# Graph-network stack on one core: eigenvector setup and layer 0 issued in one order laid out by written durations, and the second batchnorm's end moved into layer 1

## The chip, the cores and the metric

The kernel runs on one core of one Trainium2 chip. The metric is device time in microseconds (us); the time before is the median of 3 runs. One execution was also recorded by the hardware profiler, and lines quoted as "profile" are from that record. The engines are PE (TensorE matmul), PEld (TensorE weight load), DVE (VectorE), ACT (ScalarE), POOL (GpSimd) and SP (SyncE, which issues the DMAs here). All data are fp32.

## The reference

The input x is 128 graphs x 64 nodes x 256 features; all graphs share one 64 x 64 adjacency matrix `adj`. Four layers are added to x, each behind a layernorm and a relu:

```python
h = maximum(layernorm(x), 0); x = x + L0(h, adj, ...)    # and so on for L1, L2, L3

def L0(f, A, W1, b1, g1, be1, W2, b2, g2, be2):          # mix, 256 -> 512 -> 256
    A_norm = A + eye; deg = A_norm.sum(0) + A_norm.sum(1) - diagonal(A_norm)
    A_hat = A_norm * rsqrt(deg)[:, None] * rsqrt(deg)[None, :]
    agg = einsum('nm,bmd->bnd', A_hat, f).reshape(-1, 256)
    h = relu(batchnorm(agg @ W1.T + b1, g1, be1))        # statistics over all 8192 rows
    return batchnorm(h @ W2.T + b2, g2, be2)             # the same

def L1(f, A, W1, b1, W2, b2):                            # 256 -> 128 -> 256 between U.T and U
    deg = A.sum(0) + A.sum(1) - diagonal(A)
    _, U = eigh(normalised(diag(deg) - A))
    h = relu(einsum('mn,bnd->bmd', U.T, f) @ W1 + b1)
    return einsum('nm,bmd->bnd', U, h @ W2 + b2)
# L2: two adjacency layers and four LSTMs over windows of nodes; L3: attention over 512 edges
```

## The kernel before

**Tiles.** The 8192 rows are cut into 16 blocks (`NB`) of 512 rows (`BT`, 8 graphs). Block i lives in the tile `X[i]` (128 x 4 x 256) from start to end. `big` holds layer 0's intermediate results, transposed (features on the partitions).

**Eigenvectors.** `begin` issues the loads of `adj`, its transpose and x. `adjacency` (L1353) computes degrees, the scaled matrix `S` and block-diagonal copies of A_hat (`BDH`) and of the adjacency (`BDA`), which mix two graphs in one matmul. `eigenvectors` (L1398) opens the solver `Fast`: `tridiagonal` (L883) takes 62 Householder steps, c = 63 to 2, each a chain of small operations that crosses PE, ACT and DVE: two matmuls for a row and a column of A (L905, L908); a square root, reciprocals and products for `NB`; `uA`, `KAP`, `uk`, `c2`, `v` from them; a matmul that keeps the reflector's row in the PSUM tile `VM` (L929, with the one-hot tile `hot`); two outer-product matmuls (L931, L932); the next row `x` (L937) with its sum of squares; and A's update (L941). Then `scale`, `reflectors`, `values`, `twisted` and `verdict` give `U` and a flag. A branch on the flag (`tc.If(bad > 0)`) holds a slower solver `Eig`, which was not run in this execution. After it `BDU` and `BDUT` are built from U and its transpose.

**Layer 0.** `layer0` (L1538) is emitted after the solver and before the branch, so that it runs beside the solver. Its first half goes over the blocks: `norms` for four blocks at a time, relu, mix with `BDH`, eight products with W1 (`ps<-z,w`), `bn_stats` of each result (L1577) and a copy. `bn_affine` then makes scale and shift of the first batchnorm. The second half goes over the blocks again: relu with scale and shift, a reload of `X[i]` (`load_x`), eight products with W2, `bn_stats` (L1590), a copy into `big`. After the second `bn_affine` a last loop over the blocks applies scale and shift on ACT (`big<-big`), and `add_transposed` (L1519) turns the block back with 8 transposes (L1525) into two PSUM tiles `pt`, which DVE adds to `X[i]`. PSUM pools: `l0ps` with 3 buffers, `l0tps` with 2.

**Order.** Engines take their instructions in the order in which the Tile framework's scheduler emits them. Between Householder steps and layer 0's first half that order is tied by hand: `tridiagonal` collects one matmul per step in `marks`, and `pace`, called by `Kernel.mm` (L1294), makes each layer-0 product depend (an order without a semaphore) on the mark that stands for its share of the columns.

**Layer 1.** `layer1` (L1601) goes over the blocks: `norm` (four `bn_stats`, four `bn_aggr`, small operations `n_v`, `n_y`, `n_r`, `n_m`, four relus `h`), eight products `BDU,h`, two copies `a`, products with W1 (`a,w`), relu `z`, and then twice for half a block: products with W2 (`w,z`) into a tile `pt`, `y` = that + bias, the product `y,BDUT` into another `pt`, and the add to `X[i]`. The pool `l1bps` gives `pt` 4 buffers:

```python
for jj in range(0, TPB, 2):
    p = ps2.tile([P, 2, D], F32, name="pt")
```

Layers 2 and 3 follow; the change doesn't touch them. Matmuls by `Kernel.mm` show as L1295 in the profile, activations as L1300, DVE helpers as L32 to L68.

Of the kernel before, what the change touches and what calls it, by code (L numbers as in the profile page):

```python
# [11 lines left out]
ALU = mybir.AluOpType  # L12
# [774 lines left out]

class Fast:
# [7 lines left out]
    def __init__(self, tc, ctx, k):  # L796
        self.tc, self.nc, self.k = tc, tc.nc, k
        self.o = Ops(tc.nc)
        self.pool = ctx.enter_context(tc.tile_pool(name="fast", bufs=1))
        self.rows = ctx.enter_context(tc.tile_pool(name="fastr", bufs=3))  # L800
        self.ps = ctx.enter_context(tc.tile_pool(name="fastps", bufs=2, space=PSUM))
        self.psv = ctx.enter_context(tc.tile_pool(name="fastvps", bufs=1, space=PSUM))
        self.tiles = {}
        self.marks = []
# [15 lines left out]

    def after(self, later, earlier):

        self.tc.add_manual_dep(later.ins, earlier.ins.name, mybir.DependencyInfo(
            mybir.DependencyClass.NoSync, mybir.DependencyReason.DATA), reason="issue order")
        return later
# [9 lines left out]
    def constants(self):  # L835
# [22 lines left out]

        self.hot = t("hot", 1, 127)
        nc.vector.memset(self.hot[:], 0.0)  # L860
        nc.vector.memset(self.hot[:, 63:64], 1.0)
# [21 lines left out]
    def tridiagonal(self, S):  # L883
# [4 lines left out]
        o.copy(m[:], self.mm((S, self.JR[:]))[:])  # L888
        o.copy(A[:], self.mm((self.JR[:], m[:]))[:])
        NB, OA, KAP = t("NB", 64, 64), t("OA", 64, 64, 2), t("KAP", 64, 64)  # L890
        nc.vector.memset(OA[:], 1.0)
        nc.vector.memset(KAP[:], 0.0)
        nc.vector.memset(NB[:], 0.0)
        s0, r, tt, q, c2 = (t("h_" + x, 64, 1) for x in "s0 r t q c2".split())
        VM = self.psv.tile([64, 64], F32, name="fvps")
        self.VM = VM
        ja = t("ja", 64, 64)
        bc = lambda c, n=64: c.to_broadcast([n, 64])
        x = self.rows.tile([64, 65], F32, name="f_x")
        o.copy(x[:, 0:63], self.mm((bc(ident[:64, 63:64]), A[:]))[:, 0:63])  # L900
        self.act(ja[:, 0:63], x[:, 0:63], AF.Square, accum_out=x[:, 63:64])
        for c in range(63, 1, -1):
            al, h = x[:, c - 1:c], x[:, c:c + 1]
            zp = self.ps.tile([64, 64], F32, name="fps")
            nc.tensor.matmul(zp[:, 0:c], bc(ident[0:c, c - 1:c], c), A[0:c, 0:c], start=True, stop=True)  # L905
            yp = self.ps.tile([64, 64], F32, name="fps")
            self.marks.append(
                nc.tensor.matmul(yp[:, 0:c], bc(A[0:c, c:c + 1], c), A[0:c, 0:c], start=True, stop=True))  # L908
            last = self.act(s0[:], h, AF.Sqrt)
            last = self.after(self.act(OA[:, c, 1:2], al, AF.Copy), last)  # L910
            z = self.rows.tile([64, 64], F32, name="f_z")
            self.after(self.act(z[:, 0:c], zp[:, 0:c], AF.Copy), last)

            o.ts(q[:], al, **halve(0))
            o.recip(r[:], s0[:])
            o.stt(tt[:], r[:], h, s0[:], ALU.mult, ALU.add)
            nb = NB[:, c - 1:c]
            o.mul(nb, q[:], tt[:])
            uA = self.rows.tile([64, 64], F32, name="f_uA")
            o.stt(x[:, c - 1:c + 1], OA[:, c, :], nb, x[:, c - 1:c + 1], ALU.mult, ALU.add)  # L920
            o.recip(KAP[:, c:c + 1], h)
            o.stt(uA[:, 0:c], z[:, 0:c], nb, yp[:, 0:c], ALU.mult, ALU.add)
            uk = self.rows.tile([64, 64], F32, name="f_uk")
            self.act(uk[:, 0:c], x[:, 0:c], AF.Copy, scale=KAP[:, c:c + 1])
            self.sum(c2[:], uA[:, 0:c], 0.5, uk[:, 0:c], ALU.mult)
            v = self.rows.tile([64, 64], F32, name="f_v")
            o.stt(v[:, 0:c], x[:, 0:c], c2[:], uA[:, 0:c], ALU.mult, ALU.subtract)

            nc.tensor.matmul(VM[:, 0:c], self.hot[0:1, 63 - c:127 - c], x[0:1, 0:c], start=c == 63, stop=c == 2)  # L929
            p = self.ps.tile([64, 64], F32, name="fps")  # L930
            nc.tensor.matmul(p[0:c, 0:c], uk[0:1, 0:c], v[0:1, 0:c], start=True, stop=False)  # L931
            nc.tensor.matmul(p[0:c, 0:c], v[0:1, 0:c], uk[0:1, 0:c], start=False, stop=True)  # L932
            if c > 2:
                xn = self.rows.tile([64, 65], F32, name="f_x")
                w = c - 1
                o.stt(xn[:, 0:w], uk[:, 0:w], v[:, w:c], z[:, 0:w], ALU.mult, ALU.add)
                row = nc.vector.scalar_tensor_tensor(xn[:, 0:w], v[:, 0:w], uk[:, w:c], xn[:, 0:w],  # L937
                                                     op0=ALU.mult, op1=ALU.add)
                self.act(ja[:, 0:w], xn[:, 0:w], AF.Square, accum_out=xn[:, w:c])
                x = xn  # L940
            rest = nc.vector.tensor_tensor(A[0:c, 0:c], A[0:c, 0:c], p[0:c, 0:c], op=ALU.add)  # L941
            if c > 2:
                self.after(rest, row)

    def reflectors(self):
# [4 lines left out]
        nc.vector.memset(V[:], 0.0)  # L950
        self.act(V[:, 0:63], self.VM[:, 0:63], AF.Copy)
# [290 lines left out]
    def vectors(self, S, U, UT):  # L1242
        o, nc, t = self.o, self.nc, self.t
        self.tridiagonal(S)
# [36 lines left out]
class Kernel:  # L1281


    def __init__(self, tc, ctx, io):
        self.tc, self.nc, self.ctx, self.io = tc, tc.nc, ctx, io
        self.o = Ops(tc.nc)
        self.const = ctx.enter_context(tc.tile_pool(name="const", bufs=1))
        self.copies = 0
        self.pace = None
# [4 lines left out]
    def mm(self, out, lhsT, rhs, start=True, stop=True):  # L1294
        m = self.nc.tensor.matmul(out, lhsT, rhs, start=start, stop=stop)  # L1295
        if self.pace:
            self.pace(m, rhs.shape[-1])
# [55 lines left out]
    def adjacency(self):  # L1353

        nc, o = self.nc, self.o
        with ExitStack() as cx:
            pool = cx.enter_context(self.tc.tile_pool(name="adj", bufs=1))
            psum = cx.enter_context(self.tc.tile_pool(name="adjps", bufs=2, space=PSUM))
            t = lambda n, *s: pool.tile([N, *s], F32, name="a_" + n)
            I = self.ident[:N, :N]  # L1360
            self.I2 = self.c("I2", N, P)
            o.copy(self.I2[:, 0:N], I)
            o.copy(self.I2[:, N:P], I)
            rs, cs, dg, deg, junk = t("rs", 1), t("cs", 1), t("dg", 1), t("deg", 2), t("junk", N)
            o.red(rs[:], self.A[:], ALU.add)
            o.red(cs[:], self.AT[:], ALU.add)
            o.stt(junk[:], self.A[:], 1.0, I, ALU.mult, ALU.mult, acc=dg[:])
            o.add(cs[:], cs[:], rs[:])

            o.sub(deg[:, 0:1], cs[:], dg[:])  # L1370
            o.ts(deg[:, 1:2], deg[:, 0:1], 1.0, ALU.add)
            di, dm, pos = t("di", 2), t("dm", 2), t("pos", 1)
            o.ts(dm[:], deg[:], 1e-30, ALU.max)
            self.rsqrt(pool, di[:], dm[:], "a_rt")
            o.ts(pos[:], deg[:, 0:1], 0.0, ALU.is_gt)
            o.mul(di[:, 0:1], di[:, 0:1], pos[:])
            dd = t("dd", 2, N)
            for i in range(2):
                o.ts(dd[:, i, :], I, di[:, i:i + 1], ALU.mult)

            An, Ah = t("An", N), t("Ah", N)
            o.add(An[:], self.A[:], I)
            p = psum.tile([N, N], F32, name="adj_ps")
            self.mm(p[:], An[:], dd[:, 1, :])
            o.ts(Ah[:], p[:], di[:, 1:2], ALU.mult)
            self.BDH = self.block_diagonal("BDH", Ah[:], psum)
            self.BDA = self.block_diagonal("BDA", self.AT[:], psum)

            L, self.S = t("L", N), self.c("S", N, N)
            o.add(L[:], self.A[:], self.AT[:])  # L1390
            o.ts(L[:], L[:], -0.5, ALU.mult)
            o.stt(L[:], I, deg[:, 0:1], L[:], ALU.mult, ALU.add)
            p = psum.tile([N, N], F32, name="adj_ps")
            self.mm(p[:], L[:], dd[:, 0, :])
            o.ts(self.S[:], p[:], di[:, 0:1], ALU.mult)
            self.U, self.UT = self.c("U", N, N), self.c("UT", N, N)

    def eigenvectors(self, beside):  # L1398

        nc = self.nc  # L1400
        with ExitStack() as ex:
            fast = Fast(self.tc, ex, self)
            fast.constants()
            left = fast.vectors(self.S[:], self.U[:], self.UT[:])
            beside(fast)
# [6 lines left out]
        with ExitStack() as cx:  # L1412
            psum = cx.enter_context(self.tc.tile_pool(name="adjps", bufs=2, space=PSUM))
            self.BDU = self.block_diagonal("BDU", self.U[:], psum)
# [31 lines left out]
    def norms(self, pool, blocks):  # L1446

        nc, o = self.nc, self.o
# [3 lines left out]
        for k, i in enumerate(blocks):  # L1452
            for j in range(TPB):
                nc.vector.bn_stats(st[:, TPB * k + j, :], self.X[i][:, j, :])
# [743 lines left out]
```

## Time and profile before

| what | value |
|---|---|
| runs | 2451.96, 2456.36, 2457.11 us; median 2456.36 |
| profiled execution | 2457.22 us, span 2455.4 us, mean granted clock 0.986 |
| busy share of the span | PE 95%, PEld 66%, DVE 66%, ACT 46%, POOL 0% |
| first Householder matmul; last update of A | 19.56 us; ends at 292.8 us |
| flag ready on DVE | 421.8 us |
| first matmul behind the branch | 432.4 us |
| last `y,BDUT` of layer 1 | starts at 585.9 us |
| first `BDA,h` of layer 2 | 612.4 us |

How to read it: times are from the start of the span. A row of the windows gives the stretch, its length, then for PE, PEld, DVE, ACT and POOL the busy time and the number of operations, the granted TensorE clock (1.00 is full speed), the share of time that the DMA engines were busy, and GB/s. A row of the timeline gives start, length, engine, line, operation, output <- inputs, partitions x elements and count; in brackets the engine's idle time just before and what released it. One matmul of this fp32 kernel shows as two records.

### The profile page before, as it was taken

Reading aid. Unit: us, or ns where it says so; the run is one execution under the profiler, and the core shown is the slowest. Engines: PE = TensorE matmul, PEld = TensorE weight load, DVE = VectorE, ACT = ScalarE, POOL = GpSimd, SP = SyncE. Lnnn points to the kernel's source line nnn. Section 1 sums busy time; section 2 is a strip of 40 time slices with the busy share of each in tenths; the row PEclk is TensorE's granted clock in tenths of the full one; section 3 lists DMA queues with packets and bytes.
Section 4 is the critical chain, followed back from the end, with each engine's and each line's share of the span. In section 5 each row is a group of like instructions: output and inputs, shape, how many; then the busy total and the mean of one; then the engine's idle time right before and its main releaser. Section 6 shows DMA issues by size and latency. Waiting matters only on the chain.

```text
span 2455.4 us, 31930 instructions
## 1 busy us (share of the span) xinstructions
PE 2342.8 (95%) x11925; PEld 1616.8 (66%) x11925; DVE 1630.4 (66%) x4147; ACT 1117.7 (46%) x2397; POOL 2.2 (0%) x15
## 2 busy tenths in 40 slices
PE   6888899798999999999999999999999999999989
PEld 3444444564777678888899999888885444444434
DVE  7656677885653778666677676657855465756467
ACT  3555554642433565444444444335635543443321
POOL 0000000000000000000000000000000000000000
PEclk9999999898999999999999999999999999999989
DMA  5000021121101000000100002000001000000001
GB/s 155 1 1 1 24 63 53 29 75 57 35 1 13 23 1 18 1 1 1 35 1 1 1 1 69 1 1 16 1 25 45 1 5 14 14 18 13 18 14 48
DMA packets 60086, 54.77 MB, mean 22 GB/s; under 512 B 14226, under 2 KB 57747, under 8 KB 59923
## 3 DMA queue, kind: packets, MB, share of 16 engines
q1 hardware_dynamic: 59922, 52.65, 6.9%
q8 instruction: 96, 1.57, 0.3%
q14 instruction: 68, 0.55, 0.1%
HBM read 35.86 MB, written 16.78 MB: 21 GB/s over the span
## 4 chain that ended last, share of the span: by engine, by line
PE 70%; DVE 3%; issue 1%; ACT 1%; DMA 0%; DVEq 0%; ACTq 0%
PE ps L1826 39%; PE ps L1295 22%; PE acc L1295 5%; PE pt L1295 2%; PE y L1295 1%; PE ps L2007 1%; DVE X L32 0%; DVE aw L32 0%; PE ps L1525 0%; ACT ls_g L1300 0%; DVE g L32 0%; DMA ls_w<-in_L_gnn_Wih_t_dram 0%; PE pt L1525 0%; DVE ls_g L32 0%; DVE n_st L1436 0%
## 5 line engine op out<-in xcount | busy, mean ns | idle before, releaser
L1300 ACT ACTIVATE ls_g<-ls_g,ls_b 128x512 f32<-128x512 f32 (+4 forms) x472 | 243.1, 565 | 154.9 <-DVE ls_g L32 153.1
L1300 ACT ACTIVATE ls_g<-ps,ls_b 128x256 f32<-128x256 f32 (+3 forms) x268 | 115.2, 470 | 328.5 <-PE ps L1826 324.5
L1295 PE MATMUL ps<-z,w 128*128 128x512 f32 x512 | 262.4, 638 | 0.1
L32 DVE TENSOR_TENSOR aw<-at,ed_OST 128x1024 f32<-128x1024 f32 x128 | 150.0, 1219 | 93.1 <-PE ps L1295 93.0
L1826 PE MATMUL ps<-ls_tx,X 128*128 128x160 f32 (+2 forms) x960 | 206.8, 326 | 1.2 <-DVE X L32 0.7
L32 DVE TENSOR_TENSOR ls_g<-ls_z,ps 128x512 f32<-128x512 f32 (+5 forms) x256 | 146.9, 579 | 91.2 <-PE ps L1826 89.7
L1826 PE MATMUL ps<-X,X 128*128 128x160 f32 (+1 forms) x896 | 199.0, 306 | 0.0
L1826 PE MATMUL ps<-X,ls_w 128*128 128x256 f32 x640 | 190.5, 379 | 0.0
L1826 PEld LDWEIGHTS ps<-ls_tx,X 128*128 128x128 f32 x960 | 161.7, 190 | 16.0 <-DVE X L32 5.8
L1826 PE MATMUL ps<-big,X 128*128 128x160 f32 (+2 forms) x720 | 160.4, 326 | 1.5 <-ACT ls_z L1300 1.3
L32 DVE TENSOR_TENSOR X<-ls_g 128x1024 f32<-128x1024 f32 (+2 forms) x108 | 117.4, 1087 | 50.5 <-ACT ls_g L1300 50.4
L1300 ACT ACTIVATE r<-ps 128x512 f32<-128x512 f32 x256 | 129.4, 625 | 42.0 <-PE ps L1295 41.7
L1826 PEld LDWEIGHTS ps<-X,X 128*128 128x128 f32 x896 | 148.5, 190 | 0.0
L1826 PE MATMUL ps<-X,ls_s 128*128 128x256 f32 x480 | 142.3, 379 | 0.0
L1295 PEld LDWEIGHTS ps<-z,w 128*128 128x128 f32 x512 | 90.0, 195 | 72.8 <-issue 62.6
L1826 PE MATMUL ps<-ls_tx,ls_s 128*128 128x256 f32 x464 | 134.7, 379 | 0.0
L1826 PE MATMUL ps<-ls_tx,ls_w 128*128 128x256 f32 x464 | 133.4, 380 | 0.0
L1826 PE MATMUL ps<-big,ls_w 128*128 128x256 f32 x464 | 131.9, 379 | 0.7 <-ACT ls_z L1300 0.7
L1826 PEld LDWEIGHTS ps<-X,ls_w 128*128 128x128 f32 x640 | 121.4, 190 | 16.8 <-DVE X L32 0.3
L1300 ACT ACTIVATE big<-ps 128x512 f32<-128x512 f32 x96 | 69.1, 754 | 138.9 <-PE ps L1295 81.8
L1826 PEld LDWEIGHTS ps<-big,X 128*128 128x128 f32 x720 | 121.5, 190 | 14.4 <-issue 7.4
L1295 PE MATMUL ps<-ed_S,Q 64*128 64x512 f32 x512 | 128.8, 617 | 1.4 <-DVE XV L65 1.3
(506 smaller groups left out, 4156.8 us busy)
## 6 DMA issues: line engine op xcount, KB each, us to landing
X<-in_x_dram SPq DMA_DIRECT2D x32, 512.0 KB, 4.3
xs<-X SPq DMA_DIRECT2D x16, 512.0 KB, 2.9
X<-xs SPq DMA_DIRECT2D x16, 512.0 KB, 3.9
out_dram<-X SPq DMA_DIRECT2D x32, 256.0 KB, 2.1
X<-in_L_gnn_Wih_t_dram SPq DMA_DIRECT2D x4, 512.0 KB, 3.5
ls_w<-in_L_gnn_Wih_t_dram SPq DMA_DIRECT2D x4, 512.0 KB, 4.3
ls_w<-in_L_gnn_Whh_t_dram SPq DMA_DIRECT2D x4, 512.0 KB, 5.9
w<-in_L_gnn_W_t_dram SPq DMA_DIRECT2D x2, 512.0 KB, 8.6
```

The source lines that it names most:

```text
L32: self.v.tensor_tensor(o, a, b, op=op)
L1295: m = self.nc.tensor.matmul(out, lhsT, rhs, start=start, stop=stop)
L1300: self.nc.scalar.activation(out, a, f, **kw)
L1826: self.nc.tensor.matmul(out, A[m][:, x, :], Bm[m], start=first and i == 0 and j == 0, stop=i == n - 1 and j == len(parts) - 1, skip_group_ ...
L2007: self.nc.tensor.transpose(p[:, j * P:(j + 1) * P], h[:, j, dc * P:(dc + 1) * P], self.ident[:])
```

## The change

- Instructions of PE, DVE and ACT are issued through wrappers (`Ordered`, `Engines`) that, while `ordered` is set, chain each engine's instructions in the order of emission.
- A `Plan` holds one list of steps. `chain` places a step of the main path at the time that its inputs and its engine allow, by durations written in the code; `beside` queues a step that is placed into a gap before a `chain` step when it fits with a slack of 0.6 us (PE) or 0.3 us (ACT, DVE). The steps are emitted in the order of their places. The main path is `adjacency`'s way to `S` and the Householder steps; beside it are `BDH` and all of layer 0's first half (`hidden0`). `marks`, `pace` and `after` are gone.
- The `VM` matmul and `hot` are gone: each step writes its reflector's row into the SBUF tile `V` with one DMA on SP's queue. The reciprocal `KAP` is issued before `uA` instead of after it. `f_x` has 4 buffers instead of 3.
- `BDA` is built after the branch.
- Layer 0's second half is `features0`, up to the second `bn_affine`, with the order left to the scheduler. `l0ps` has 5 buffers instead of 3; `l0tps` is gone.
- The last loop of layer 0 becomes `end0(i)`, called at the head of block i in `layer1`, with its transposes in `l1bps`, that is in the tiles `pt` of layer 1.

The core of the diff:

```diff
+class Ordered:
+        def call(*a, **kw):
+            i = method(*a, **kw)
+            if self.owner.ordered:
+                if self.last is not None:
+                    self.owner.tc.add_manual_dep(i.ins, self.last.ins.name, mybir.DependencyInfo(
+                        mybir.DependencyClass.NoSync, mybir.DependencyReason.DATA), reason="issue order")
+                self.last = i
+            return i
...
+class Plan:
+    def start(self, x):
+        needs, at = list(x.needs), self.free[x.engine]
+        if x.bank is not None and len(self.opened) >= self.banks:
+            needs += self.opened[-self.banks]
+        for y in needs:
+            if y.at is None:
+                return None
+            at = max(at, y.at + y.ready)
+        return at
+
+    def fill(self, engine, until):
+        while True:
+            best = None
+            for x in self.queue[engine][:12]:
+                at = self.start(x)
+                if at is not None and at + x.busy <= until + self.slack[engine] and (best is None or at < best[0]):
+                    best = at, x
+            if best is None:
+                return
+            self.queue[engine].remove(best[1])
+            self.place(best[1], best[0])
+
+    def chain(self, engine, emit, needs=(), busy=0.09, ready=0.22):
+        x = Step(engine, emit, needs, busy, ready, None)
+        self.fill(engine, max([y.at + y.ready for y in needs], default=0.0))
+        self.place(x, self.start(x))
+        return x
...
-            nc.tensor.matmul(VM[:, 0:c], self.hot[0:1, 63 - c:127 - c], x[0:1, 0:c], start=c == 63, stop=c == 2)
...
+        def row_uk():
+            nc.sync.dma_start(V[c:c + 1, 0:c], now["x"][0:1, 0:c])
+            now["uk"] = self.rows.tile([64, 64], F32, name="f_uk")
+            self.act(now["uk"][:, 0:c], x(0, c), AF.Copy, scale=KAP[:, c:c + 1])
...
+        z = go("T", zy, [rest], 0.34, 0.42)
+        sq = go("S", lambda: self.act(s0[:], x(c, c + 1), AF.Sqrt), [h], 0.13, 0.23)
...
+        d = go("V", lambda: o.recip(KAP[:, c:c + 1], x(c, c + 1)), [d])
+        uk = go("S", row_uk, [d], 0.16, 0.32 + e)
+        d = go("V", row_uA, [zs, b, z], 0.12 + e, 0.25 + e)
...
     def eigenvectors(self):
+            plan = Plan(dict(T=0.6, S=0.3, V=0.3), 5)
+            made, mixes = self.adjacency(fast, plan)
+            self.open0(ex)
+            self.hidden0(plan, mixes)
+            fast.tridiagonal(self.S[:], made, plan)
+            nc.ordered = True
+            plan.emit()
+            nc.ordered = False
+            left = fast.vectors(self.U[:], self.UT[:])
+            plan.rest()
+            plan.emit()
+            self.features0()
             bad = nc.values_load(left[0:1, 0:1], min_val=0, max_val=64)
...
+            self.BDA = self.block_diagonal("BDA", self.AT[:], psum)
             self.BDU = self.block_diagonal("BDU", self.U[:], psum)
...
+    def hidden_block(self, i, r, m, plan, needs, used):
...
+            x = beside("T", lambda hc=hc: product(hc, 0), mixed, 0.86, 0.9, bank)
+            x = beside("T", lambda hc=hc: product(hc, 1), [x], 0.86, 1.0)
+            used[i].append(x)
+            bank.append(beside("V", lambda hc=hc: nc.vector.bn_stats(self.st1[:, hc, i, :], now["p", hc][:]), [x],
+                               0.62, 0.7))
+            bank.append(beside("S", lambda hc=hc: self.act(self.hidden(i, hc), now["p", hc][:], AF.Copy),
+                               [x] + h, 0.55, 0.65))
...
-            for i in range(NB):
-                for oc in range(2):
-                    self.act(self.part(i, oc), self.part(i, oc), AF.Identity,
-                             scale=sc2[:, oc:oc + 1], bias=sh2[:, oc:oc + 1])
-                self.add_transposed(pst, i, lambda dc, j: self.part(i, dc)[:, j * P:(j + 1) * P])
...
+    def end0(self, i, psum):
+        sc2, sh2 = self.affine2
+        for oc in range(2):
+            self.act(self.part(i, oc), self.part(i, oc), AF.Identity, scale=sc2[:, oc:oc + 1], bias=sh2[:, oc:oc + 1])
+        self.add_transposed(psum, i, lambda dc, j: self.part(i, dc)[:, j * P:(j + 1) * P])
...
     def layer1(self):
             for i in range(NB):
+                self.end0(i, ps2)
                 h = self.norm(pool, i)
```

## The prediction

> **What bounds the kernel now.** The sum is made against the profiled execution: 2457.2 us, of which the span is 2455.4; the median of the runs, 2456.4, lies 0.8 lower. About 0.2% (5 us) is what a measurement of this kernel can tell from no change.
>
> First the windows by stage. The columns are the stretch, its length, then busy time and count for PE, PEld, DVE, ACT and POOL, the granted clock, the DMA share and GB/s.
>
> ```profile
> 20.00:293.00 273.00, 232.13 (x1133) 122.54 (x1132) 184.06 (x968) 145.74 (x539) 0.00 (x0) 0.97 0.05 15
> 293.00:432.00 139.00, 132.35 (x391) 58.24 (x391) 106.67 (x445) 70.59 (x122) 0.00 (x0) 0.98 0.21 62
> 432.00:456.00 24.00, 16.29 (x95) 12.10 (x96) 19.80 (x52) 19.71 (x29) 0.00 (x0) 0.79 0.06 18
> 456.00:586.00 130.00, 124.70 (x554) 83.04 (x553) 99.16 (x342) 57.65 (x117) 0.74 (x3) 0.99 0.19 63
> ```
>
> The rows are the Householder steps beside layer 0's first half; the values beside its second half; the 128 transposes that end layer 0; layer 1. PE is 85, 95, 68 and 96% busy. Layer 1 has no slack on PE, and gets there by overlapping blocks. That is seen in its timeline (start, length, engine, line, operation, count, idle before):
>
> ```profile
> 573.73 1.13 PE L1295 MATMUL pt<-w,z 128*128 128x256 f32 x4
> ...
> 574.70 1.05 PE L1295 MATMUL ps<-BDU,h 128*128 128x128 f32 x8
> 574.90 0.69 DVE L32 TENSOR_TENSOR y<-pt,w_b 128x512 f32<-128x512 f32 x1 [0.26 <-PE pt L1295]
> ...
> 575.64 1.12 PE L1295 MATMUL pt<-y,BDUT 128*128 128x512 f32 x2
> ...
> 576.81 0.69 DVE L32 TENSOR_TENSOR X<-X,pt 128x512 f32<-128x512 f32 x1 [1.22 <-PE pt L1295]
> ```
>
> While DVE makes y, PE works at another block's BDU,h: the wait from w,z to y,BDUT (1.91 us) costs PE little, because a later block's norm is ready. Next the clock around the branch, in windows with the same columns:
>
> ```profile
> 428.00:432.00 4.00, 0.44 (x2) 0.00 (x0) 0.70 (x1) 0.60 (x1) 0.00 (x0) 1.00 0.01 4
> 432.00:436.00 4.00, 1.09 (x4) 0.93 (x4) 3.21 (x17) 0.20 (x1) 0.00 (x0) 0.53 0.29 82
> 436.00:440.00 4.00, 2.39 (x9) 1.62 (x10) 1.38 (x5) 3.51 (x5) 0.00 (x0) 0.50 0.05 19
> 440.00:444.00 4.00, 3.57 (x20) 2.92 (x19) 3.83 (x9) 4.00 (x7) 0.00 (x0) 0.69 0.00 0
> ```
>
> Behind 4 us without PE work the clock stands at half, and it is full again only near 443, 5 us after the transposes began at 437.4.
>
> **Start.** The first Square stands at 20.15 us, behind S at 17.44. The new order puts adjacency first: A lands at 2.96; some 17 small DVE operations, a square root and seven dependent operations at 0.15 to 0.2 bring S to about 8.3; the 2.7 from S to Square stay. 11.0 instead of 20.15: -9.
>
> **Householder steps.** 62 steps from 20.0 to 292.6 are 4.40 us each. Timeline of one of them:
>
> ```profile
> 101.69 1.12 PE L1295 MATMUL ps<-z,w 128*128 128x512 f32 x2
> ...
> 102.74 0.28 PE L931 MATMUL fps<-f_v,f_uk 1*47 1x47 f32 x2
> ...
> 103.40 0.31 PE L905 MATMUL fps<-f_A,ident 46*64 46x46 f32 x2 [0.29 <-DVE f_h_q L47]
> ```
>
> The step's matmuls stand behind layer-0 products; the dependent operations alone add up to 3.19 in this stretch (v to x 0.29, x 0.29, square 0.30, root 0.36, NB 0.23 + 0.19 + 0.25, x 0.26, KAP 0.22, uk 0.18, c2 0.38, v 0.24). The built order of the changed kernel has four steps without products (3.19 each, and about 4 for the first 16 bn_stats of 0.36 that stand among them: 17), 45 that carry all of layer 0's first half, two without (bn1; 8.5 together), 11 with second-half products. The 45: PE needs 8 products x 0.86 + 2 mixes x 0.98 = 8.84 per block, 141 us for 16, 3.14 per step, with 0.65 for the step's own matmuls 3.8; small misfits of DVE and ACT make it 4.15, 187 us. The 11: about 45, 4.1 each. 11 + 17 + 187 + 8.5 + 45 = 268, rounded down to 266 since the last steps are short. Gain 27, the start's 9 included. Bounds: 3.8 per filled step and 3.2 at the end give 243 (gain 50); one product of 0.86 too many in each of the 45 gives 305 (loss 12).
>
> The VM matmul becomes one DMA per step on SP. Its x tile returns four steps (16 us) later, and the slowest DMA kind in the page's list lands after 8.6: hidden, 0. V's last row lands some 2 us late, beside `scale`.
>
> **Values.** DVE's chain took 129.2 us (292.6 to 421.8). It loses 8 of 28 bn_stats (-3.4) and takes the layer-3 edge work and X0's adds (+9.5) which stood behind the branch: 135, and 4 to the branch: 139 as before (139.8). All second affines lie before the branch too, on ACT, in the twisted loop. If that cover is gone they cost 32 x 0.73 = 23 at most. The branch moves from 432.4 to about 405.4.
>
> **Layer 1.** This decides. Each block's head now has two X adds and 8 transposes, into the `pt` ring that layer 1's w,z and y,BDUT use. Ring tiles are handed out in program order, so the built order puts the transposes of block i+1 behind the last y,BDUT of block i; its norm needs those adds, and its BDU,h the norm. On PE, DVE and ACT the 16 blocks stand strictly one after the other: nothing fills the links. The links, from the start of a last y,BDUT, by rows of layer 1, the transposes and the norms at 605 to 612:
>
> - X add +1.17, next block's two X adds 0.60 apart; bn_stats at 2.97 (the transposes, 1.16 for eight, end at 2.1 under these adds);
> - four bn_stats and aggr, n_v at 4.70; n_y 0.17, reciprocal 0.24, five operations at 0.19: n_m at 6.07; first h at 6.25, four relus 0.51 apart, last ready at 8.36;
> - BDU,h and copy a to 10.40; a,w to z 1.06; z to w,z 0.74; w,z to y 1.17; y to y,BDUT 0.74: 14.11;
> - second w,z +0.97, y +1.06, y,BDUT +0.74: 16.9.
>
> So P = 16.9 us per block at full clock, though PE has only 7.45 + 1.16 = 8.6 to do. PE idles from 2.1 to about 7 in each block, longer than the 4 us that halved the clock above. The matmuls in the chain during the 5 us of recovery, half of BDU,h (1.05) and a,w (0.86), take as long again, with a little of w,z: +2.1, P = 19.0. Bounds: +0, and all the chain's matmuls at half clock, +6.4, P = 23.3.
>
> [...]
>
> Before, 153.5 us lay between the branch and the last y,BDUT (432.4 to 585.87), transposes included. After, block 0's transposes lie before the branch; its bn_stats start some 2.1 us behind the branch, 2.97 into a period: 16 P - 0.9. The loss is 16 P - 154.4, at 19.0 us 150. The rest of the kernel keeps its order. Sum: 2457.2 - 27 + 150 = 2580.
>
> **Rivals.**
> - The clock stays full, P = 16.9: loss 116, 2546. For it: small gaps elsewhere in the Householder stage leave the mean clock at 0.97.
> - The clock stays at half, P = 23.3: loss 218, 2649. For it: PE would be half idle. Against it: near 443 the clock was restored by transposes that left PE idle a fifth of the time.
> - The Householder steps do not shorten (the written durations miss, each engine waits in turn): 2607.
> - Other side, faster: blocks overlap as before, a few ahead; then PE's 8.6 per block is the price, 16 x 8.6 - 154.4 = -17, with -27: 2413. Place: layer 1 alone; it decides below P = 11.3, where 16 P - 154.4 = 27. Against it stands the built order, which holds no matmul of block i+1 ahead of block i's last.
>
> **How the numbers follow.** Forecast 0.50, full clock 0.25, half clock 0.10, no Householder gain 0.10, overlap 0.05. The range 2520 to 2640 runs from the full clock with the Householder gain near its bound (2523) to the forecast with a small Householder loss or P near 22; it leaves out the overlap and most of the half-clock case. Faster 0.05, within 0.2% 0.01, slower 0.94.
>
> **What would show it.** Right: last Householder add near 266, branch near 405, layer 1 with PE about half busy, BDU,h of a block 9 us behind the previous y,BDUT, clock of 0.6 to 0.8 there. Wrong: PE over 75% busy in layer 1, or BDU,h between w,z and y,BDUT of another block; a Householder end past 292.

## The result and the profile after

The changed kernel takes 2591.3 us (median of 4 runs, 2589.9 to 2592.2), the kernel before 2456.6; the ratio is 1.0552, 95% interval 1.0534 to 1.0570. Slower was forecast, at 2580. The profiled execution took 2589.9 us, its span is 2588.1: 132.7 more than the span before. In the table a stage ends at the start of the operation named; "predicted" is from the text above.

| event (us from the span's start) | before | predicted | after |
|---|---|---|---|
| first square of a Householder row | 20.15 | 11.0 | 11.35 |
| last update of A | 292.6 | 266 | 285.6 |
| first matmul behind the branch | 432.4 | 405.4 | 421.6 |
| last `y,BDUT` of layer 1 | 585.9 | 708.5 | 721.0 |
| from the branch to it | 153.5 | 303.1 | 299.4 |
| first `BDA,h` of layer 2 | 612.4 | not given | 746.6 |
| from there to the end | 1843.0 | the same | 1841.5 |

So 10.8 us are gained up to the branch, layer 1 loses 145.9, and the rest differs by -2.4: 132.7. In the changed kernel nearly all instructions show as L798, the line of the wrapper that issues them. First the windows, with the columns as above: the Householder steps, the values, layer 1, four pieces of one period of layer 1, and the stretch at half clock of the period behind it.

```profile
15.40:286.00 270.60, 247.33 (x1099) 126.48 (x1100) 198.53 (x998) 173.47 (x577) 0.00 (x0) 0.98 0.13 37
...
286.00:421.00 135.00, 89.43 (x302) 40.87 (x300) 107.72 (x472) 63.59 (x112) 0.74 (x3) 0.84 0.12 34
421.00:721.00 300.00, 181.22 (x640) 118.61 (x640) 118.23 (x355) 57.03 (x112) 0.00 (x0) 0.85 0.09 28
...
498.00:503.00 5.00, 0.09 (x1) 0.09 (x1) 3.64 (x17) 0.94 (x3) 0.00 (x0) 1.00 0.31 105
503.00:506.00 3.00, 3.00 (x13) 2.95 (x14) 0.69 (x1) 1.34 (x3) 0.00 (x0) 0.50 0.00 0
506.00:509.00 3.00, 2.60 (x9) 1.05 (x7) 0.00 (x0) 0.96 (x2) 0.00 (x0) 0.93 0.00 0
509.00:516.00 7.00, 5.06 (x20) 2.97 (x20) 2.77 (x5) 0.32 (x1) 0.00 (x0) 1.00 0.00 0
...
520.10:526.90 6.80, 5.66 (x19) 4.58 (x20) 1.02 (x3) 2.67 (x5) 0.00 (x0) 0.50 0.00 0
```

PE's share in layer 1 went from 96 to 60%, and part of that 60% is half clock: each period has 5 us without PE work, and near their end the clock falls to 0.50, for 3.4 us in this period (503.0 to 506.4) and for 6.8 in the next. No other engine took PE's place as the bound; all three wait in turn. The values stage is 66% PE now, with DVE the busiest at 80%. The timeline of one period shows the links (start, length, engine, line, operation, count, idle before):

```profile
502.26 2.08 ACT L798 ACTIVATE h<-X,n_m,n_r 128x256 f32<-128x256 f32 x4 [1.30 <-DVE n_m L798]
...
502.91 3.81 PE L798 MATMUL ps<-BDU,h 128*128 128x128 f32 x16 [5.17 <-ACT h L798]
...
509.38 1.13 PE L798 MATMUL pt<-w,z 128*128 128x256 f32 x4 [0.78 <-ACT z L798]
510.54 0.69 DVE L798 TENSOR_TENSOR y<-pt,w_b 128x512 f32<-128x512 f32 x1 [4.63 <-PE pt L798]
...
511.29 1.12 PE L798 MATMUL pt<-y,BDUT 128*128 128x512 f32 x2 [0.79 <-DVE y L798]
...
514.06 1.13 PE L798 MATMUL pt<-y,BDUT 128*128 128x512 f32 x2 [0.78 <-DVE y L798]
...
515.02 1.04 PE L798 MATMUL pt<-ident,big 128*128 128x128 f32 x8
```

Between `w,z` and `y,BDUT` stood another block's BDU,h before; now PE idles there (0.79), and for 5.17 us ahead of BDU,h, released by the relu `h` of the same block. The next block's transposes (515.02) stand behind the last product of this one. The DVE rows `n_m`, one per block, stand 18.31 and 19.23 us apart in turn, 18.8 on average; the longer period is the one with 6.8 us at half clock.

### The profile page after: what moved, and what is told of

It is laid out like the page before. It is cut to its first block, busy times and chain, and to the rows that moved or that the text cites. A ratio compares the mean times of both kernels' runs of the same rounds, so it can differ in the third digit from the quotient of the medians.

```text
span 2588.1 us, 31946 instructions
## 1 busy us (share of the span) xinstructions
PE 2355.6 (91%) x11801; PEld 1627.5 (63%) x11801; DVE 1639.5 (63%) x4145; ACT 1118.8 (43%) x2396; POOL 2.2 (0%) x15
## 4 chain that ended last, share of the span: by engine, by line
PE 67%; DVE 3%; ACT 0%; issue 0%; DMA 0%; SPq 0%; DVEq 0%; ACTq 0%
PE ps L798 59%; PE acc L798 5%; PE pt L798 2%; DVE sm_m L798 1%; PE y L798 1%; DVE X L798 0%; DVE aw L798 0%; DVE n_st L798 0%; ACT ls_g L798 0%; DVE g L798 0%; DVE ls_g L798 0%; DMA X<-in_L_gnn_Wih_t_dram 0%; DMA ls_w<-in_L_gnn_Wih_t_dram 0%; DVE sm_e L798 0%; DVE ls_s L798 0%
## 5 line engine op out<-in xcount | busy, mean ns | idle before, releaser
L798 ACT ACTIVATE ls_g<-ls_g,ls_b 128x512 f32<-128x512 f32 (+4 forms) x472 | 243.1, 565 | 154.6 <-DVE ls_g L798 152.6
L798 ACT ACTIVATE ls_g<-ps,ls_b 128x256 f32<-128x256 f32 (+3 forms) x268 | 115.2, 470 | 328.7 <-PE ps L798 324.8
L798 PE MATMUL ps<-z,w 128*128 128x512 f32 x512 | 254.8, 624 | 0.0
L798 PE MATMUL ps<-big,X 128*128 128x176 f32 (+3 forms) x848 | 212.8, 366 | 0.5 <-ACT ls_z L798 0.4
L798 DVE TENSOR_TENSOR aw<-at,ed_OST 128x1024 f32<-128x1024 f32 x128 | 149.8, 1218 | 92.3 <-PE ps L798 92.3
L798 PE MATMUL ps<-ls_tx,X 128*128 128x160 f32 (+2 forms) x960 | 206.7, 326 | 1.2 <-DVE X L798 0.6
L798 DVE TENSOR_TENSOR ls_g<-ls_z,ps 128x512 f32<-128x512 f32 (+5 forms) x256 | 146.6, 578 | 91.5 <-PE ps L798 90.0
L798 PE MATMUL ps<-X,X 128*128 128x160 f32 (+1 forms) x896 | 199.0, 306 | 0.0
L798 PE MATMUL ps<-X,ls_w 128*128 128x256 f32 x640 | 190.4, 379 | 0.0
L798 PEld LDWEIGHTS ps<-ls_tx,X 128*128 128x128 f32 x960 | 161.8, 190 | 15.9 <-DVE X L798 5.5
L798 PEld LDWEIGHTS ps<-big,X 128*128 128x128 f32 x848 | 145.9, 190 | 30.5 <-issue 19.4
L798 DVE TENSOR_TENSOR X<-ls_g 128x1024 f32<-128x1024 f32 (+2 forms) x108 | 117.4, 1087 | 50.9 <-ACT ls_g L798 50.8
L798 PEld LDWEIGHTS ps<-X,X 128*128 128x128 f32 x896 | 148.5, 190 | 0.0
L798 ACT ACTIVATE r<-ps 128x512 f32<-128x512 f32 x256 | 129.4, 625 | 41.8 <-PE ps L798 41.7
L798 PE MATMUL ps<-X,ls_s 128*128 128x256 f32 x480 | 142.3, 379 | 0.0
L798 PE MATMUL ps<-BDU,h 128*128 128x128 f32 x256 | 62.1, 436 | 81.9 <-ACT h L798 81.9
L798 PE MATMUL ps<-ls_tx,ls_s 128*128 128x256 f32 x464 | 134.7, 379 | 0.0
L798 PEld LDWEIGHTS ps<-z,w 128*128 128x128 f32 x512 | 88.8, 192 | 72.5 <-issue 63.6
L798 PE MATMUL ps<-ls_tx,ls_w 128*128 128x256 f32 x464 | 133.3, 380 | 0.0
L798 PE MATMUL ps<-big,ls_w 128*128 128x256 f32 x464 | 131.9, 380 | 0.7 <-ACT ls_z L798 0.7
L798 PEld LDWEIGHTS ps<-X,ls_w 128*128 128x128 f32 x640 | 121.4, 190 | 16.8 <-DVE X L798 0.3
L798 PE MATMUL ps<-ed_S,Q 64*128 64x512 f32 x512 | 128.6, 617 | 1.4 <-DVE XV L798 1.3
```

Source lines behind the costliest of these rows:

```text
L798: i = method(*a, **kw)
```

## The experiments

**Theory.** The end of the second batchnorm in layer 1 makes layer 1 serial, because its transposes share the ring `pt` (the 4 buffers of that pool, handed out in turn) with layer 1's products and so stand behind the block before; the clock that falls in the gap costs some 2 us per block; the rest of the change gains. **Rivals:** the written order itself slows the kernel; the place in the program makes it serial, not the ring; the clock costs nothing and the links are only longer than the rows said. Ratios are to the kernel before, run on the same chip.

### Layer 1

`e1_end0_first`: the loop goes back ahead of layer 1, the rest of the change stays.

```diff
+            cx0, (pst,) = self.stage([("l0tps", 2)])
+            with cx0:
+                for i in range(NB):
+                    self.end0(i, pst)
             self.layer1()
...
-                self.end0(i, ps2)
```

> Edit: the changed kernel, but all 16 end0 calls stand ahead of layer 1, in a PSUM pool of their own (as before the change); everything else of the change stays. Theory 1 (end0 at the block's head, through the shared ring, makes layer 1 serial at P = 18.8 us per block): layer 1 falls from 299.5 us, branch to last y,BDUT, to about 150 (153.5 before the change), and the time from 2591 to about 2445, some 11 below the kernel before, which is what the Householder and values part gains. Rival (the loss sits in the static order or in a clock that the new order leaves low for the whole stage): layer 1 stays above 200 us, the time above 2500.

Measured: 2437.5 us, ratio 0.9932 (0.9909 to 0.9955); branch to last `y,BDUT` 148.6 us, layer 1's PE full again (97% busy from 447 to 571 us).

`e2_own_ring`: the same place, another ring.

```diff
-        cx, (w, pool, psum, ps2) = self.stage([("l1w", 1), ("l1", 2), ("l1ps", 4), ("l1bps", 4)])
+        cx, (w, pool, psum, ps2, pst) = self.stage([("l1w", 1), ("l1", 2), ("l1ps", 3), ("l1bps", 3), ("l1tps", 2)])
...
-                self.end0(i, ps2)
+                self.end0(i, pst)
```

> Edit: end0 stays at the head of each block of layer 1, but its transposes get a ring of their own (2 buffers; l1ps and l1bps have 3 instead of 4). Theory 1 with the ring as the cause: the transposes no longer wait for y,BDUT, blocks overlap, layer 1 takes 130 to 155 us, the time is 2425 to 2450. Rival (the place in the program alone makes it serial: norm(i+1) is emitted behind block i): P stays near 18.8, 2590. A second rival: 3 buffers instead of 4 hold layer 1 back, 160 to 200 us, 2450 to 2490.

Measured: 2435.4 us, ratio 0.9927 (0.9904 to 0.9949). All 128 transposes now stand ahead of the branch, which moves to 437.5, and layer 1 takes 127.6 us. So neither the place in the program nor 3 buffers cost much: the shared ring did.

`e3_two_ahead`: the shared ring, two blocks of lead.

```diff
-                self.end0(i, ps2)
+                for k in (range(3) if i == 0 else range(i + 2, min(i + 3, NB))):
+                    self.end0(k, ps2)
```

> Edit: the shared ring stays, but end0 is called two blocks ahead (blocks 0 to 2 ahead of block 0, then block i+2 at the head of block i). Theory 1 in the form of the chain (what costs is that block i+1's norm hangs on transposes behind block i's last product): with two blocks of lead the norm is ready in time, P falls to PE's or DVE's own work, 8.6 to 10 us, layer 1 to 140 to 160, the time to 2430 to 2455. Rival (sharing 4 buffers among six tiles per block is the cost by itself, whatever the lead): P above 12, the time above 2490.

Measured: 2433.8 us, ratio 0.9921 (0.9898 to 0.9944); layer 1 takes 142.1 us, 8.9 per block with its start counted in. The window of that stage:

```profile
424.00:566.00 142.00, 132.66 (x625) 91.81 (x625) 109.64 (x351) 55.94 (x112) 0.00 (x0) 0.96 0.18 59
```

PE is at 93%, with the same work in half the time. Six tiles per block in four buffers are no cost by themselves; what cost is that a ring hands out its tiles in program order, and that the norm hung on a tile handed out behind the last product of the block before.

`e5_before_moved`: the kernel before, with this part of the change alone.

```diff
-            sc2, sh2 = self.bn_affine(w, "bn2", st2, b2, g2, be2)
-            for i in range(NB):
-                ...
+            self.affine2 = self.bn_affine(self.const, "bn2", st2, b2, g2, be2)
...
             for i in range(NB):
+                self.end0(i, ps2)
                 h = self.norm(pool, i)
```

> Edit: the kernel before, with only one part of the change: the second batchnorm's scale, shift, transposes and adds go to the head of each block of layer 1, through the shared ring; adjacency, Householder steps and layer 0 stay as they were. Theory: this part alone makes layer 1 serial: from the branch to the last y,BDUT 295 to 305 us instead of 153.5, the time 2457 + 146 = 2600, give or take 8. Rival (the serial layer 1 needs the changed kernel's emission order): under 2500.

Measured: 2608.3 us, ratio 1.0629 (1.0608 to 1.0650); branch to last `y,BDUT` 307.9 us, in the same periods of 18.31 and 19.23. The loss needs nothing else of the change. The 8.5 us over layer 1 of the changed kernel lie at its start, where the second batchnorm's scale and its first block still come behind the branch: the first `y,BDUT` follows it after 24 us instead of 15.

### The clock

`e4_warm`: 44 transposes of the identity more per block, in a `ps` tile that nothing reads.

```diff
                 self.end0(i, ps2)
+                p = psum.tile([P, BT], F32, name="ps")
+                for k in range(44):
+                    self.nc.tensor.transpose(p[:, k % 4 * P:(k % 4 + 1) * P], self.ident[:], self.ident[:])
```

> Edit: the changed kernel with 44 more transposes of the identity per block in layer 1, into a ps tile that nobody reads; the scheduler puts 21 of them (about 3 us) behind a block's 8 transposes, where PE idles, and the rest into the waits for z and y. Theory 1 with the clock term (P = 16.9 at full clock, the rest of 18.8 is half clock behind the gap): granted clock in layer 1 near 1.00, P near 16.9, the time falls by 16 x 1.9 = 30 to about 2561. Rival (the links are longer than the rows said, and the clock costs nothing): the same or slower than 2591.

Measured: 2583.6 us, ratio 1.0529 (1.0505 to 1.0553); 8 less, not 30; the interval overlaps that of the changed kernel, and layer 1 in the profile is 5.1 us shorter (294.3). Neither side was right as written. Two blocks of its timeline:

```profile
503.13 3.65 PE L798 MATMUL ps<-BDU,h 128*128 128x128 f32 x16 [2.88 <-ACT h L798]
...
521.90 2.19 PE L798 MATMUL ps<-BDU,h 128*128 128x128 f32 x16 [2.89 <-ACT h L798]
```

After the same pause the 16 records took 3.65 us in one block, near the 3.81 of the changed kernel (502.91, where the windows read 0.50), and 2.19 in another, about twice the 1.05 that eight take in the kernel before (574.70, in a window at 0.99): behind a pause of 2.9 us the products came once at about half rate and once at full. The granted clock is 0.92 from 424 to 716 us, where the changed kernel has 0.86 from 424 to 721. Three of fifteen periods are 17.36 or 17.37 us, the others 18.5 to 19.1.

`e6_warm_gap`: all 44 in the gap, by taking the extra tile from the shared ring and by tying PE, DVE and ACT to the order of emission from there to the mix with BDU. The diff is to `e4_warm`.

```diff
-                p = psum.tile([P, BT], F32, name="ps")
+                p = ps2.tile([P, 2, D], F32, name="pt").rearrange("p a b -> p (a b)")
+                self.nc.ordered = True
...
                 self.mix(psum, h, self.BDU, lambda dc, p: self.move(a[:, dc, :], p[:]))
+                self.nc.ordered = False
```

> Edit: the changed kernel with the 44 extra transposes per block in a tile of the shared ring, so that all 44 (44 x 0.117 = 5.1 us at full clock) stand in the gap between a block's 8 transposes and its BDU,h. The run before filled 2.5 us of that gap and left pauses of 2.9 us, and the clock still fell in most blocks; where it did not, the period was 17.36 us. Theory (the clock is the whole difference between 17.36 and 18.8): with no pause over 1 us the granted clock is 0.97 or more in layer 1, the periods are 17.3 to 17.6, the time is 2591 - 16 x 1.3 = 2570. Rival (what lengthens most periods is not the pause but the order or the DMA beside it): periods of 18.5 remain, 2585 to 2595.

Measured: 2570.5 us, ratio 1.0482 (1.0462 to 1.0503). Fourteen of fifteen periods are 17.32 to 17.38 us, layer 1 takes 277.9. Its window:

```profile
424.00:700.00 276.00, 228.46 (x1292) 163.46 (x1292) 116.65 (x353) 57.03 (x112) 0.00 (x0) 0.98 0.09 31
```

More work on PE and a shorter stage: 17.36 us is the chain, and the clock, 0.98 here, the other 1.4. The tied order alone was not run, but `e4_warm`, which has none in layer 1, shows the same 17.36 us in its three short periods.

### Householder steps and values

The branch came 16.2 us later than predicted: the last update of A is 19.6 late, and the values stage makes up 3.4. These runs stand on `e3_two_ahead` (2433.8), where layer 1 no longer hides anything. In the changed kernel, SP's queue is long at the start (start, length, engine, line, operation, count, idle before):

```profile
16.91 5.42 SPq L1475 DMA_DIRECT2D X<-in_x_dram  x3
...
32.37 9.05 SPq L1038 DMA_DIRECT2D f_V<-f_x  x6
34.34 0.27 DVE L798 SCALAR_TENSOR_TENSOR f_x<-f_uk,f_v,f_z 64x59 f32<-64x59 f32 x1 [6.70 <-DMA f_V<-f_x]
```

The first reflector rows wait behind the loads of x and of layer 0's weights until 32.4, and step c = 60, which writes the first x tile again, waits 6.70 us for them.

`e7_poolq`:

```diff
-            nc.sync.dma_start(V[c:c + 1, 0:c], now["x"][0:1, 0:c])
+            nc.gpsimd.dma_start(V[c:c + 1, 0:c], now["x"][0:1, 0:c])
```

> Edit: on the kernel with end0 two blocks ahead (2433.8): the 62 DMAs of the reflector rows are issued from POOL's queue instead of SP's, where they stand behind the loads of x and of layer 0's weights until 32.4 us. Theory (the 10.39 us of step c = 60 holds a wait of 6.7 us for the x tile that such a DMA reads): the step falls to 4, all later times move by -6, the time to about 2428. Rival (layer 0's first products need the same 6 us anyway, since their weights and norms come no earlier): the Householder end stays at 285, the time at 2434. Second rival: POOL's DMAs slow DVE; steps get longer everywhere, above 2440.

Measured: 2432.4 us, ratio 0.9919 (0.9905 to 0.9933), no difference from 0.9921 that this can tell. The step c = 60 fell from 10.19 to 3.99 us, but c = 59 and 58 grew from 3.56 and 6.38 to 5.20 and 7.70 (layer 0's first products, with PE busy throughout from 33 to 42 us and at first at half the later rate: a pair of `ps<-z,w` records takes 2.08 us at 33.53 and 1.13 at 41.23; in the changed kernel, where a pair takes 2.08 at 38.30, the clock column reads 1.00 from 36.0 to 40.9, so the clock is not shown as the reason), and c = 12 by 0.65: the last update of A comes 2.6 earlier, the branch 2.9. The wait was real, and more than half of it stood ahead of another one.

`e8_hold`: no W2 product ahead of the last outer product (`done`).

```diff
-                    self.mm(p[:], W2[:, kc, oc * P:(oc + 1) * P], z[:, kc, :], kc == 0, kc == 3)
+                    x = nc.tensor.matmul(p[:], W2[:, kc, oc * P:(oc + 1) * P], z[:, kc, :], start=kc == 0, stop=kc == 3)
+                    self.tc.add_manual_dep(x.ins, done.ins.name, ...)
```

> Edit: on the kernel with end0 two blocks ahead (2433.8): no W2 product of layer 0 may be issued ahead of the last outer product of the Householder steps (50 of 128 were). Theory (PE's products make the last 11 steps 4.9 us each; bare they take 3.0 to 3.2): the Householder end falls from 285 to about 264, the values stage has 50 x 0.86 = 43 us more PE work beside 89 of 135, still just covered by DVE's chain, and the branch comes 15 to 20 us earlier: 2414 to 2420. Rival (the products only move: PE then bounds the values stage): the branch stays near 423, 2430 to 2436.

Measured: 2429.4 us, ratio 0.9908 (0.9895 to 0.9921). The last eleven steps fell from 4.3 to 5.6 (the first 8.5) to between 2.95 and 4.17, eight of them 3.0 or less; the last update of A from 285.4 to 267.2 and the branch from 423.6 to 407.3, as expected. But layer 1 took 153.5 us instead of 142.1. Why, its timeline shows just behind the branch:

```profile
407.31 0.40 PE L798 MATMUL adj_ps<-AT,I 64*128 64x64 f32 x2 [3.78 <-DVEq L1571]
...
411.67 0.16 DVE L798 TENSOR_TENSOR bn_sh<-bn_sh,w_be 128x2 f32<-128x2 f32 x1
...
411.87 8.57 ACT L798 ACTIVATE big<-big,bn_sh,bn_sc 128x512 f32<-128x512 f32 x12 [3.00 <-DVE bn_sh L798]
```

The W2 products ended only behind the flag (396.9), so the second batchnorm's shift came at 411.67, behind the branch, and its 32 affines (scale and shift on ACT) lost the cover of the solver's `twisted` stage. Of 16 us gained, 11 came back there.

`e9_poolq_hold`: both edits.

> Both edits of the two runs before it. If each theory holds, 2408 to 2414; if only the queue counts, 2428; if neither, 2434.

Measured: 2424.9 us, ratio 0.9889 (0.9873 to 0.9905). Branch at 402.4, layer 1 153.5: it misses its 2408 to 2414 by the same 11 us.

`e11_hold_part`: as `e9_poolq_hold`, with the products of blocks 0 and 1 free.

```diff
+                    if i > 1:
+                        self.tc.add_manual_dep(x.ins, done.ins.name, ...)
```

> Edit: on the kernel with POOL's queue and the held W2 products (2424.9), only the products of blocks 2 to 15 are held; the 16 of blocks 0 and 1 may go into the last Householder steps. Theory (holding all moved the bound of the values stage to PE: 10.5 us lay between the flag and the first matmul behind the branch, against 5): 16 x 0.86 = 14 us of PE work leaves that stage, the Householder end rises by 5 to 7, and the net is 0 to -5: 2420 to 2425. Rival (every product in the steps costs its full time there): 2430.

Measured: 2421.3 us, ratio 0.9867 (0.9850 to 0.9883), the fastest here; its interval overlaps the one of `e9_poolq_hold`. The last update of A comes 8.5 later (271.0), the branch 3.1 (405.5), layer 1 takes 148.5 instead of 153.5. The Householder end was expected to rise by 5 to 7, the time to be 2420 to 2425.

`e10_no_order`: the emission order of the plan stays, the chains that enforce it go.

```diff
-            nc.ordered = True
             plan.emit()
```

> Edit: on the kernel with end0 two blocks ahead (2433.8): the plan still sets the order of emission, but the chains that tie each engine to it are left out, so that the scheduler may move instructions. In its order the filled steps carry 4 to 5 products instead of 3 to 4, and W2 products start at c = 24 instead of c = 12. Theory (steps are bound by the PE work put into them): 33 steps of some 5 us and 23 of 4.3 give a Householder end near 305 instead of 285; the values stage then has less PE work but is bound by DVE's chain, 136 us, so the branch comes 15 to 20 us later: 2448 to 2455. Rival (written order is worth nothing): 2430 to 2438.

Measured: 2462.8 us, ratio 1.0035 (1.0022 to 1.0049); 29 more than with the chains. The last update of A is at 321.1, 16 later than expected: 10 of its loss is the start, which I had not thought of (the first update of A is at 25.5 instead of 15.4, since the scheduler puts other work ahead of adjacency again), 25.5 are the fuller steps. The values stage is then 8.5 shorter. So the order is worth its 29 us against this scheduler on its own; against the hand-tied order of before it is the start that gains, not the steps: from first to last update of A it is 266.5 us before and 270.2 after, though the steps now also carry some 50 W2 products that were in the values stage before.

## Why the prediction was right

**Layer 1, the deciding step, held.** The serial order was read from the built kernel, and `e1_end0_first`, `e2_own_ring`, `e3_two_ahead` and `e5_before_moved` each show that the ring makes it. P was 19.0 and is 18.8; 16 P - 0.9 gives 299.9 with it, and 299.4 were measured. Its two terms were each off, and that 19.0 lies so near is partly luck, since their errors (+0.5 and -0.7) cancel: the chain at full clock is 17.36 us (16.9 predicted; some links were short by 0.05 to 0.15, as `n_v` to `n_m`, 1.52 instead of 1.37, and `n_m` to `h`, 0.25 instead of 0.18), the clock costs 1.4 (2.1 predicted). The 2.1 was an estimate from the 5 us at half clock behind the branch; the two stretches at half clock read in layer 1 are 3.4 and 6.8 us long. It went by a pause of 4 us; in `e4_warm` BDU,h took 3.65 us instead of 2.19 already behind one of 2.88. That nothing fills the links held: PE stood idle for 5.0 to 5.2 us ahead of BDU,h in each block behind the first.

**Start: right.** 11.0 was predicted for the first square, 11.35 measured.

**Householder steps: the terms that were mis-sized.** A gain of 27 was summed up to the last update of A (the terms below, 268, rounded to 266), and 7.0 came. By its own terms:

| term | predicted | measured |
|---|---|---|
| up to the last update ahead of the filled steps | 28 | 34.8 |
| 45 filled steps | 187 | 189.7 |
| two without products | 8.5 | 7.2 |
| the last 11 | 45 | 53.9 |

The first row is the reflector DMA, put at nothing: I took the time to landing from the issue (8.6 against 16 us) and left out what stands ahead of it on SP's queue. With that wait gone (`e7_poolq`) only 2.6 us come back, since the next two steps and c = 12 grow.

The last row is PE work that was priced too low. These steps hold nearly all of the 50 W2 products that `e8_hold` moves; at the prediction's own 0.86 each, with 0.65 per step for the step's matmuls, that is 50 us, not 45. Two windows of the changed kernel show the rest:

```profile
226.50:236.80 10.30, 6.29 (x22) 3.04 (x23) 6.21 (x43) 6.83 (x21) 0.00 (x0) 0.50 0.21 52
236.80:286.00 49.20, 49.20 (x179) 20.50 (x178) 28.45 (x148) 33.73 (x100) 0.00 (x0) 1.00 0.26 76
```

From 236.8 on PE is never idle: a step with four W2 products takes 4.32, not 4.1, and c = 10 and 9, with five to six, take 5.19 and 5.63. The step c = 12 took 8.52: it holds six, and the first of them ran at half clock (a pair of records takes 2.08 us at 231.54 and 1.12 at 240.07). Ahead of it PE had paused for 3.2 us in step c = 14, a wait that the profile puts down to the first batchnorm's `bn_v`, and then for 2.0.

**Values: right.** 139 predicted, 136.0 measured; the affines lay beside the `twisted` stage as said, and `e8_hold` shows the price when they do not (11 us; 23 had been named as the most).

**The sum and the signs.** The 2580 was too low by 11 and not by more because the 19.6 us that the last update of A came late were partly made up: 3.4 in the values stage, 3.7 in layer 1, 2.4 behind it. Of the signs named, PE at 60% fits "about half busy", but the clock in layer 1 is 0.85, not 0.6 to 0.8, and BDU,h starts 7.2 us behind the previous block's last y,BDUT (514.06 to 521.24), not 9; the prediction's own links, with the first `h` at 6.25, fit 7 and not 9.

**The rivals.** Full clock (2546) is refuted by the 0.85 of the stage, half clock throughout (2649) by the 1.00 at the end of a period (509.0 to 516.0); the transposes said to have restored the clock near 443 left PE idle for 5% of 437.4 to 443.0, not for a fifth. No Householder gain (2607) was the nearest: the steps gained nothing, the start and the values did. Overlap (2413) is what `e3_two_ahead` makes, with P = 8.9 under the break-even of 11.3: 2433.8.

## What to carry to other kernels

Moving a loop's work into the head of the next loop was free here only where the built order let it run ahead of the block before (2433.8 us in `e3_two_ahead`, 2591.3 in the changed kernel): check the built order of each engine for the first instruction of block i+1 that stands behind the last of block i, and whose tile ring put it there. The chain of links, summed from the trace's rows, was then the price per block (17.36 us at a clock of 0.98), not PE's busy time (8.6 by the prediction's rows). For a DMA that is added to each step, count what is queued ahead of it at its first issues (a wait of 6.70 us here), and what work moves behind a branch when other work is delayed (11 us in `e8_hold`).

## What the runs showed of the hardware

- Behind a pause of 2.88 us on PE the 16 records of BDU,h took 3.65 us in one block, and behind one of 2.89 us they took 2.19 in another (`e4_warm`). What decides between the two is not shown. Extra work in the gap, which nobody reads, made the stage 21.5 us shorter, at a granted clock of 0.98 (424 to 700 us) instead of 0.86 (424 to 721) (`e6_warm_gap`): 44 transposes per block that cost less than the pause.
- The alternation of 18.31 and 19.23 us periods, block by block, stands in the changed kernel and in `e5_before_moved` alike, in the changed kernel with a pause of 5.0 to 5.2 us ahead of BDU,h from block 1 on; in `e6_warm_gap`, at 0.98, it is gone (17.32 to 17.38 us in fourteen of fifteen periods). The stretch at half clock that starts near the end of the pause is 3.4 us in the shorter period and 6.8 in the longer (503.0 to 506.4 and 520.1 to 526.9 in the changed kernel). What sets the phase was not tried.
